# Values projected per pixel row and spread into windows by DRAM transfers, and the norm's square with one PSUM operand, in a fused attention and mixture-of-experts kernel

## The chip, the cores and the metric

The kernel runs on one core of a Trainium2 chip. A core has five engines with a queue each, executed in order: TensorE (PE in the profile; its weight loads are PEld), VectorE (DVE), ScalarE (ACT), GpSimd (POOL) and SyncE (SP), which here only issues transfers (its queue is SPq). Transfers run on 16 DMA engines [...]. The working memory SBUF has 128 partitions; TensorE writes its results to PSUM. The metric is the device time of one execution in microseconds (us). Before the change it is 4484.66 us, the median of three runs (4481.55 to 4487.19). The profiled execution spans 4480.1 us.

## What is computed

The input `x` has the shape (2, 128, 256, 256): two images of 128 channels. A block of attention is added to it, then a block of experts. All is float32. Cut to what matters:

```python
# attention block: windows of 8x8 pixels attend to 12x12 pixels around them, 4 heads of 32
xn  = (x - mean_c(x)) / sqrt(var_c(x) + 1e-6)         # norm over the 128 channels of a pixel
q, k, v = split(W_qkv @ xn)
k, v = unfold_windows(k), unfold_windows(v)           # 12x12 patches with step 8, zeros outside
attn = softmax(q * SCALE @ k.T + rel_pos_emb(q) + FIXED_MASK)
x    = x + W_out @ (attn @ v)
# experts, for each pixel as a token t
t = x.reshape(2, 128, -1).transpose(0, 2, 1)
n = (t - mean(t)) / sqrt(var(t) + 1e-5)
p = softmax(n @ router_w + router_b);  p2, i2 = top_k(p, 2);  p2 = p2 / sum(p2)
out = t + sum_k p2[k] * (n @ expert_w[i2[k]] + expert_b[i2[k]])
```

`FIXED_MASK` removes every second row and every second column offset. So a pixel attends only to pixels of the same parity of row and column: each image falls into four independent planes of half height and half width, and in a plane a window of 4x4 pixels attends to 6x6 pixels. That is why the halo on each side is one pixel of the plane.

## The kernel before

**Tiling.** An image is cut into 32 strips of 8 rows, 64 strips in all. Each strip has four planes (row parity by column parity), 256 planes in all, and the main loop (L779) runs over them. A plane has 4 rows by 128 columns of pixels, 512 tokens, in 32 windows. The window rows of a strip need six plane rows: four of its own and one above and below. Six rows are kept as a ring: `place(i, k)` says in which of six places row `k` of strip `i` lies, and the two rows that two strips share stay where they are. `ln_rows(i)` gives the rows that strip `i` has to bring in anew: rows 2 to 5 inside an image, 1 to 5 in its first strip and 2 to 4 in its last. `runs` groups such rows into stretches of neighbouring places.

**The values.** Two neighbouring windows read 10 columns of the plane (KC): 8 of their own and one of halo on each side. So 16 column groups of 6 x 10 = 60 pixels, in slots of 64, cover the plane, and the halo columns are in two groups each. GpSimd copies the normalized pixels `xn` into this doubled order (`columns`, L331) as `xcol`, with 128 partitions of channels; two groups (half 0 and half 1) stand side by side and fill 128 pixels. TensorE then multiplies each of the eight pairs of groups by `wv` (`values`, L369), four pairs into one PSUM tile, and ScalarE copies the tile into `vv` (L376): pixels on the partitions, channels along the row, as the attention (L496) needs them. Per plane that is eight matmuls of 128x128 by 128x128 and two ScalarE copies. A float32 matmul shows as two records in the trace, so four matmuls are the "x8" in a row of the timeline.

**The keys** are not doubled before the projection: `pk` is projected once per pixel (L396), and ScalarE doubles the halo columns while it copies out of PSUM into `kcol` (L407, L414), which lasts from strip to strip in the ring.

**The order.** The loop is a software pipeline whose order is written out by hand: under `tc.manual_schedule` each engine executes its instructions in the order in which the Python code emits them. Several planes are in work at once. For iteration `n`: scores of plane `n` (L448, L465; exp at L473), the projection of plane `n + 1` (the generator `ahead` = `project`: first value group, `pu`, `pk`, `pq`), the last four expert products of one pixel-row pair (`ex.product`, L686), the attention of plane `n` (L486, L496; division by the sums at L506 to L516), the norm statistics of two later pixel-row pairs (`norms`, L554 to L572), the second value group, three expert products, the output projection `po` (L524, added to `xt` at L529), the fourth product. VectorE's order around the change: the expert multiplies `xe` (L677), `ex.end` (L692), the attention's `sT`, `rc`, `rT`, `o` (L506 to L516), the transposed statistics `plg` (L563), `rstd` (L228 to L235), the gates of the router (`route`, L587 to L619) up to `gT` (L625), then `uT` (L386) and `au` (L354).

**The norm.** `rstd` takes mean and mean square of the pixels from the PSUM tile `plg`, as views `mean` and `sq`. L228 copies the mean to the SBUF tile `r`, L229 squares it, L230 subtracts from `sq`, L231 clamps and adds epsilon (`epsc` lies in SBUF), ScalarE does Ln and Exp (L232, L233), L234 and L235 make a Newton step.

**GpSimd** does, per plane: a marker `last` (L681) that makes it wait for VectorE's sixth expert multiply, expert multiply 5 (L677), the normalization of one pixel-row pair (`ln1`, L272), every fourth plane the copy of a shared row (`halo`, L246), expert multiply 7 (L677), and `columns` of a plane two ahead (L331).

**SyncE** issues all transfers of the loop in order: eight broadcasts of gates per plane (`gb`, L661), one each of `sb` and `rb` (L666, L637), one load of `x` (L115), one store (L722) and two small writes of the gates to DRAM (`gd`, L633), from which `gb`, `sb` and `rb` are read back. The expression `nc.scalar` or `dve` in `fetch` names the engine whose little write into the tile marks when the transfer may start. PSUM has three rotating tiles of one bank for everything that `mm_tile` asks for.

Of the kernel before, what the change touches and what calls it, by code (L numbers as in the profile page):

```python
# [11 lines left out]
F32 = mybir.dt.float32  # L12
AF = mybir.ActivationFunctionType
ALU = mybir.AluOpType
# [3 lines left out]
P = 128  # L18
# [25 lines left out]
KR, KC = 6, 10  # L44
NK = KR * KC
SLOT = 64
# [5 lines left out]
def kernel(  # L52
# [39 lines left out]
    def mm_tile(name):  # L92
        return ps_mm.tile([P, 512], F32, tag="mm", name=name)

    def ctile(shape, name):
        return const.tile(shape, F32, tag=name, name=name)
# [98 lines left out]
    nc.tensor.matmul(pr[:, :P], lhsT=wall[:, 0, :], rhs=relbd, start=True, stop=True)  # L195
    nc.vector.tensor_copy(wrel, pr[:, :P])

    xn, xcol, kcol = [], [], []
    for i in range(2):
        xn.append(ctile([P, 2, 2, KR, PC + 2], f"xn{i}"))  # L200
        nc.gpsimd.memset(xn[i][:, :, :, :, 0 : PC + 2 : PC + 1], 0.0)
    for i in range(4):
        xcol.append(ctile([P, HP, 2, SLOT], f"xcol{i}"))
        kcol.append(ctile([P, NP, SLOT], f"kcol{i}"))
        nc.gpsimd.memset(xcol[i][:, :, :, NK:], 0.0)
        nc.gpsimd.memset(kcol[i][:, :, NK:], 0.0)
        nc.gpsimd.memset(kcol[i][:, 0, 0:NK:KC], 0.0)
        nc.gpsimd.memset(kcol[i][:, NP - 1, KC - 1 : NK : KC], 0.0)
# [9 lines left out]
    def rstd(p4, k0, k1, name):  # L218

        u, r = (
            small.tile([P, 2, NT], F32, tag=v, name=f"{v}_{name}")[:, k0:k1] for v in ("u", "r")
        )
        mean, sq = (
            p4[:, :, E + 2 * k0 + j : E + 2 * k1 : 2].rearrange("p t k -> p k t") for j in range(2)
        )
        nc.vector.tensor_copy(r, mean)  # L228
        nc.vector.tensor_tensor(u, r, r, ALU.mult)  # L229
        nc.vector.scalar_tensor_tensor(u, u, -1.0, sq, ALU.mult, ALU.add)  # L230
        nc.vector.scalar_tensor_tensor(u, u, 0.0, epsc[:, k0:k1], ALU.max, ALU.add)  # L231
        nc.scalar.activation(r, u, AF.Ln, scale=4.0)  # L232
        nc.scalar.activation(r, r, AF.Exp, scale=-0.5)  # L233
        nc.vector.scalar_tensor_tensor(u, u, -4.0, r, ALU.mult, ALU.mult)  # L234
        nc.vector.tensor_tensor(u, u, r, ALU.mult)  # L235
        return r, u

    def ln_rows(i):

        s = strips[i][1]  # L240
        return range(1 if s == 0 else 2, KR - 1 if s == NS - 1 else KR)
# [9 lines left out]
    def place(i, k):  # L251

        return (PR * strips[i][1] + k) % KR

    def runs(i, rows):

        out = []
        for k in rows:
            if out and place(i, k) == out[-1][1] + out[-1][2]:
                out[-1][2] += 1  # L260
            else:
                out.append([k, place(i, k), 1])
        return out
# [59 lines left out]
            ln1(i, k, pb, nc.vector)  # L323
        yield

    def columns(n):

        i, pl = divmod(n, 4)
        for k, at, m in runs(i, ln_rows(i)):
            for half in range(2):  # L330
                nc.gpsimd.tensor_copy(  # L331
                    xcol[pl][:, :, half, at * KC : (at + m) * KC].rearrange(
                        "p t (r c) -> p t r c", c=KC
                    ),
                    windows(xn[i % 2][:, pl // 2, pl % 2, k : k + m], half * HP, HP),
                )
        for k, s in ((0, 0), (KR - 1, NS - 1)):
            if strips[i][1] == s:
                c0 = place(i, k) * KC
                nc.gpsimd.memset(xcol[pl][:, :, :, c0 : c0 + KC], 0.0)  # L340
                nc.gpsimd.memset(kcol[pl][:, :, c0 : c0 + KC], 0.0)

    def shift(uT, n, state):

# [12 lines left out]
    def project(n, state):  # L357
# [1 line left out]
        i, pl = divmod(n, 4)  # L359
        xp = xn[i % 2][:, pl // 2, pl % 2]  # L360
        inner = xp[:, 1 : 1 + PR, 1 : PC + 1]
        xl, kk = xcol[pl], kcol[pl]

        vv = work.tile([P, HP, P], F32, tag="vv", name=f"vv{n}")

        def values(t0):
            pv = mm_tile(f"pvv{n}_{t0}")
            for t in range(4):
                nc.tensor.matmul(  # L369
                    pv[:, t * P : (t + 1) * P],  # L370
                    lhsT=xl[:, t0 + t].rearrange("p a k -> p (a k)"),
                    rhs=wv,
                    start=True,
                    stop=True,
                )
            nc.scalar.copy(vv[:, t0 : t0 + 4, :].rearrange("p t c -> p (t c)"), pv)  # L376

        values(0)
        yield

        pu = mm_tile(f"pu{n}")
        nc.tensor.matmul(pu, lhsT=wrel, rhs=inner, start=True, stop=True)  # L384
# [37 lines left out]
        )  # L422
        yield

        values(4)
        state.update(qs=qs, kk=kk, vv=vv)
        yield

    def windows(rows, n0, count):

        first = rows[:, :, 8 * n0 : 8 * n0 + KC].unsqueeze(1)
        dims = [list(d) for d in first.ap]
        dims[1] = [8, count]
        return bass.AP(first.tensor, first.offset, dims)
# [310 lines left out]
            next(part)  # L745
    if len(strips) > 1:
        halo(1)
    columns(0)
    states = {0: {}}
    for _ in project(0, states[0]):  # L750
        pass
    states[0]["shift"]()
    if n_planes > 1:
        columns(1)

# [20 lines left out]
    with tc.manual_schedule(engines={ET.PE, ET.DVE, ET.Activation, ET.Pool, ET.SP}):  # L778
        for n in range(n_planes + 7):  # L779
# [32 lines left out]
            next(ahead, None)  # L812
            if n + 1 < n_planes:
                states[n + 1]["shift"]()
            next(ahead, None)
            next(ahead, None)
            for e in (4, 6, 7, 5):
# [26 lines left out]
            new.fetch(3, dve)  # L844
            while to_store:
                store(*to_store.pop())
            next(ahead, None)
            ex.product(0)
            made = next(norm, None)
# [8 lines left out]
                halo(i + 2)  # L858
            nxt.times(7, pool)
            if n + 2 < n_planes:  # L860
                columns(n + 2)
            next(outp, None)
            ex.product(3)
            next(outp, None)
# [61 lines left out]
```

The softmax here doesn't subtract the row's maximum and nothing guards it: scores larger than these inputs give would overflow.

## Time and profile before

| what | value |
|---|---|
| time, median of 3 | 4484.66 us |
| VectorE square L229, planes 0 to 259 | 0.16 to 1.30 us, median 0.83, sum 233.0 |
| L228, the copy before it | 0.17 us, sum 44.0 |
| value matmuls L369, 4096 records | 594.3 us busy, 288 ns each |
| ScalarE copy L376, 512 | 299.8 us, 586 ns each |
| GpSimd copy L331, 672 | 237.6 us, 391 ns each |
| GpSimd expert multiply L677, 512 | 650.8 us, 1272 ns each |
| `gb` transfers L661, 2048 of 256 KB | issue 0.32 us, landing after 4.0 |
| `rb` transfers L637, 249 of 256 KB | issue 0.33 us, landing after 3.3 |
| `gd` writes L633, 516 of 16 KB | issue 0.59 us, landing after 3.0 |
| stores L722, 256 of 256 KB | issue 0.43 us, landing after 4.2 |
| DMA packets, main queue | 517,568, 58.3% of the time of 16 engines |

The page gives for each engine the time in which an instruction was running. A busy TensorE is not one at its peak, since matmuls overlap; the time that a group of them holds the engine is read from the start of the first to the start of what follows. The timeline has columns start, duration, engine, line, operation, output and inputs, shapes, and how many instructions were merged; idle time before the instruction and what ended it stand in brackets. A duration includes a wait that arises inside the engine once the instruction has been issued. A wait for a semaphore shows as idle time before it.

### The profile page before, as it was taken

What the parts mean: (1) busy time and instruction counts of PE and PEld (TensorE: products, weight loads), DVE (VectorE), ACT (ScalarE), POOL (GpSimd) and SP (SyncE); (2) the same over time, 40 slices, a digit from 0 to 9 for tenths busy, and PEclk for the clock granted to TensorE, in tenths of its full rate; (3) what the DMA queues carried; (4) which work ended last, traced back from release to release, by engine and by line L of the source; (5) the groups of instructions that cost most, each with busy time, mean ns of one, the idle gap of its engine ahead of it and who ended that gap; (6) DMA issues with size and microseconds to landing.
All of it is one profiled execution on the core that took longest, in us unless ns stands there. A gap on an engine that the chain in (4) does not pass through costs nothing. (4 is left out here: it accounts for less than half of the span.)

```text
span 4480.1 us, 224632 instructions
## 1 busy us (share of the span) xinstructions
PE 4422.6 (99%) x96321; PEld 2683.3 (60%) x96321; DVE 3996.2 (89%) x11850; ACT 1467.7 (33%) x4022; POOL 1317.7 (29%) x1815
## 2 busy tenths in 40 slices
PE   7999999999999999999999999999999999999997
PEld 5666666666666666666666666666666666666653
DVE  5899999999899999998989999999999999989887
ACT  3333333333333333333333333333333333333321
POOL 1232323232323233232323232323232323232321
PEclk9999999999999999999999999999999999999999
DMA  2565666566656666666666566666665666566655
GB/s 83 174 191 185 192 185 192 186 191 185 193 184 192 185 191 187 189 188 188 189 187 189 187 190 185 193 183 193 184 193 185 192 185 192 186 191 186 190 164 186
DMA packets 519284, 828.12 MB, mean 185 GB/s; under 512 B 124186, under 2 KB 125850, under 8 KB 518298
## 3 DMA queue, kind: packets, MB, share of 16 engines
q1 hardware_dynamic: 517568, 813.46, 58.3%
q8 instruction: 769, 12.60, 1.1%
q14 instruction: 217, 1.78, 0.2%
q10 hardware_dynamic: 730, 0.29, 0.0%
HBM read 737.95 MB, written 75.56 MB: 182 GB/s over the span
## 5 line engine op out<-in xcount | busy, mean ns | idle before, releaser
L686 PE MATMUL acc<-xe,ew 128*128 128x512 f32 x4096 | 1889.0, 594 | 19.6 <-DVE gb L660 18.8
L686 PEld LDWEIGHTS acc<-xe,ew 128*128 128x128 f32 x4096 | 758.8, 190 | 885.7 <-issue 861.8
L677 DVE TENSOR_TENSOR xe<-xs,gb 128x512 f32<-128x512 f32 x1536 | 950.9, 687 | 10.2 <-PE acc L686 0.7
L681 POOL COPY last<-xe 128x1 f32<-128x1 f32 x256 | 47.9, 187 | 3060.8 <-DVE gb L660 3054.6
L376 ACT COPY vv<-pvv 128x512 f32<-128x512 f32 x512 | 299.8, 586 | 1395.7 <-PE pvv L369 1379.6
L677 POOL TENSOR_TENSOR xe<-xs,gb 128x512 f32<-128x512 f32 x512 | 650.8, 1272 | 5.9 <-PE att L496 2.5
L369 PE MATMUL pvv<-wt,xcol 128*128 128x128 f32 x4096 | 594.3, 288 | 2.5 <-POOL xcol L331 1.5
L369 PEld LDWEIGHTS pvv<-wt,xcol 128*128 128x128 f32 x4096 | 496.4, 191 | 64.8 <-issue 51.8
L272 POOL TENSOR_TENSOR xn<-xt,rb 128x512 f32<-128x512 f32 x249 | 375.0, 1506 | 66.5 <-DMA rb<-gd 55.9
L465 PE MATMUL att<-qs,kcol 32*64 32x32 f32 x32768 | 392.4, 226 | 0.8 <-issue 0.7
L465 PEld LDWEIGHTS att<-qs,kcol 32*64 32x64 f32 x32768 | 391.0, 130 | 1.0 <-issue 1.0
L496 PEld LDWEIGHTS att<-pT,vv 64*32 64x32 f32 x32768 | 348.0, 105 | 39.4 <-issue 2.5
L496 PE MATMUL att<-pT,vv 64*32 64x32 f32 x32768 | 343.2, 200 | 2.3 <-issue 2.3
L473 ACT ACTIVATE pT<-att 128x1024 f32<-128x1024 f32 x256 | 261.9, 1023 | 243.1 <-PE att L465 239.7
L548 ACT ACTIVATE sq<-xt 128x512 f32<-128x512 f32 x505 | 292.7, 631 | 0.0
L354 DVE STREAM_TRANSPOSE au<-auT 128x512 f32<-128x512 f32 x256 | 269.2, 1052 | 9.0
L524 PE MATMUL po<-o,wt 128*128 128x512 f32 x512 | 262.0, 593 | 6.1 <-DVE o L516 3.2
L384 PE MATMUL pu<-xn,wrel 128*128 128x512 f32 x512 | 262.5, 594 | 0.0
L407 ACT COPY kcol<-pk 128x560 f32<-128x560 f32 (+2 forms) x344 | 174.1, 506 | 268.2 <-PE pk L396 265.3
L418 PE MATMUL pq<-xn,wt 128*128 128x512 f32 x512 | 262.0, 593 | 0.0
L396 PE MATMUL pk<-xn,wt 128*128 128x512 f32 (+2 forms) x528 | 261.0, 578 | 0.0
L386 DVE STREAM_TRANSPOSE uT<-pu 128x512 f32<-128x512 f32 x256 | 182.8, 714 | 78.0 <-PE pu L384 77.0
(2697 smaller groups left out, 5243.8 us busy)
## 6 DMA issues: line engine op xcount, KB each, us to landing
gb<-gd SPq DMA_DIRECT2D x2048, 256.0 KB, 4.0
xt<-in_x_dram SPq DMA_DIRECT2D x256, 256.0 KB, 4.9
sb<-gd SPq DMA_DIRECT2D x256, 256.0 KB, 3.5
out_dram<-xt SPq DMA_DIRECT2D x256, 256.0 KB, 4.2
rb<-gd SPq DMA_DIRECT2D x249, 256.0 KB, 3.3
gd<-gT SPq DMA_DIRECT2D x516, 16.0 KB, 3.0
ew<-in_L_ffn_expert_w_dram SPq DMA_DIRECT2D x1, 512.0 KB, 5.0
eb<-in_L_ffn_expert_b_dram SPq DMA_DIRECT2D x1, 512.0 KB, 5.7
```

What stands on the lines that cost most here:

```text
L272: eng.tensor_tensor(xn[i % 2][:, :, :, k, 1 : PC + 1], ln1_src(i, k).rearrange("p (y j x) -> p y x j", y=2, x=2), rb.rearrange("p (y j x) ...
L354: nc.vector.transpose(au.rearrange("p m a s -> p a s m"), auT[n % 2])
L369: nc.tensor.matmul(pv[:, t * P : (t + 1) * P], lhsT=xl[:, t0 + t].rearrange("p a k -> p (a k)"), rhs=wv, start=True, stop=True,)
L376: nc.scalar.copy(vv[:, t0 : t0 + 4, :].rearrange("p t c -> p (t c)"), pv)
L384: nc.tensor.matmul(pu, lhsT=wrel, rhs=inner, start=True, stop=True)
L418: nc.tensor.matmul(pq, lhsT=wq, rhs=inner, start=True, stop=True)
L465: nc.tensor.matmul(sc[rows, h, 32 * t : 32 * t + 32], lhsT=kk[hp, half * HP + t, :], rhs=qs[hp, m0 : m0 + 2].rearrange("p m a s -> p (m a ...
L496: nc.tensor.matmul(av[hp, half, 32 * t : 32 * t + 32], lhsT=vv[rows, t, hp], rhs=pT[rows, h, 32 * t : 32 * t + 32], start=True, stop=True,)
L524: nc.tensor.matmul(po, lhsT=wo, rhs=state["o"].rearrange("p f z -> p (f z)"), start=True, stop=True)
L548: nc.scalar.activation(sq, src, AF.Square)
L677: eng.tensor_tensor(self.xe[e], self.xs, self.gb.pop(e), ALU.mult)
L686: nc.tensor.matmul(self.acc, lhsT=ew[:, e, :], rhs=self.xe.pop(e), start=(e == 0), stop=not self.xe)
```

## The change

There are two edits.

**Values once per pixel.** `columns`, `xcol` and the second value group go. `value_rows` projects every new plane row once: one matmul per row, with the 128 pixels of the row as stationary operand, so that the pixels come out on the partitions. ScalarE copies the tile to SBUF (`vr`). `send_values` writes it to a DRAM buffer `vrows` (one per plane, six rows in the ring, 130 columns of which the outer two stay zero, 128 channels), and `take_values` reads it back as overlapping windows: for each new row and half one transfer of 10 partitions (columns) by 8 windows by 128 channels, 40 KB in pieces of 512 B, into `vwin`, which stays from strip to strip as `kcol` does. `borders` does what was left of `columns`: zeros for rows outside the image. The purpose is to project no halo pixel twice, and to let the transfers do the doubling that GpSimd did.

**The square.** L229 multiplies the copy `r` by the PSUM view `mean` instead of by itself. The value is the same; one operand is read from PSUM.

```diff
+    zero = ctile([P, 2, P], "zero")
...
     for i in range(4):
-        xcol.append(ctile([P, HP, 2, SLOT], f"xcol{i}"))
+        vwin.append(ctile([P, HP, P], f"vwin{i}"))
         kcol.append(ctile([P, NP, SLOT], f"kcol{i}"))
+        vrows.append(dram.tile([KR, PC + 2, P], F32, tag=f"vrows{i}", name=f"vrows{i}", bufs=1))
+        nc.gpsimd.memset(vwin[i], 0.0)
+        nc.sync.dma_start(vrows[i][:, 0 : PC + 2 : PC + 1, :], zero[0:KR])
...
-        nc.vector.tensor_tensor(u, r, r, ALU.mult)
+        nc.vector.tensor_tensor(u, r, mean, ALU.mult)
...
-    def columns(n):
...
+    def value_rows(n):
+        i, pl = divmod(n, 4)
+        xp = xn[i % 2][:, pl // 2, pl % 2]
+        rows, sent = list(ln_rows(i)), []
+        for part in (rows[-4:], rows[:-4]):
+            if not part:
+                continue
+            pv = mm_tile(f"pv{n}_{part[0]}")
+            m = len(part)
+            for j, k in enumerate(part):
+                nc.tensor.matmul(pv[:, j * P : (j + 1) * P], lhsT=xp[:, k, 1 : PC + 1], rhs=wv,
+                                 start=True, stop=True)
+            vr = work.tile([P, 4, P], F32, tag="vr", name=f"vr{n}_{part[0]}")
+            nc.scalar.copy(vr[:, 0:m].rearrange("p r c -> p (r c)"), pv[:, : m * P])
+            sent.append((part, vr))
+        return sent
+    def send_values(n, sent):
+        i, pl = divmod(n, 4)
+        for part, vr in sent:
+            for k, at, m in runs(i, part):
+                nc.sync.dma_start(vrows[pl][at : at + m, 1 : PC + 1, :].rearrange("r c d -> c r d"),
+                                  vr[:, k - part[0] : k - part[0] + m])
+    def take_values(n):
+        i, pl = divmod(n, 4)
+        s = strips[i][1]
+        for k in range(0 if s == 0 else 2, KR):
+            at = place(i, k)
+            for half in range(2):
+                p0 = half * SLOT + at * KC
+                src = vrows[pl][at, half * HP * 8 : half * HP * 8 + KC, :].unsqueeze(1)
+                dims = [list(d) for d in src.ap]
+                dims[1] = [8 * P, HP]
+                nc.sync.dma_start(vwin[pl][p0 : p0 + KC], bass.AP(src.tensor, src.offset, dims))
...
-        values(0)
-        yield
...
+        state["sent"] = value_rows(n)
+        yield
...
-        values(4)
-        state.update(qs=qs, kk=kk, vv=vv)
+        state.update(qs=qs, kk=kk, vv=vwin[pl])
         yield
...
                 states[n + 1]["shift"]()
+                send_values(n + 1, states[n + 1]["sent"])
...
             while to_store:
                 store(*to_store.pop())
+            if n + 1 < n_planes:
+                take_values(n + 1)
             next(ahead, None)
             ex.product(0)
...
             if n + 2 < n_planes:
-                columns(n + 2)
+                borders(n + 2)
```

So the sends of plane `n + 1` stand in SyncE's queue behind `spread` (`gd` and `rb`) and ahead of `sb`, and its takes behind the store and ahead of the fetches of `gb` 4 and 6.

## The prediction

> **What bounds the kernel now.** I read the busy line first, then one window over the steady stretch, then the waits, then the timeline of single planes. The busy line and the window (columns: length, then busy time of PE, PEld, DVE, ACT, POOL, then clock, DMA share, GB/s):
>
> ```profile
> PE 4422.6 (99%) x96321; PEld 2683.3 (60%) x96321; DVE 3996.2 (89%) x11850; ACT 1467.7 (33%) x4022; POOL 1317.7 (29%) x1815
> ...
> 180.00:4300.00 4120.00, 4119.93 (x90232) 2502.24 (x90231) 3731.25 (x11041) 1371.11 (x3758) 1240.61 (x1670) 1.00 0.61 188
> ```
>
> TensorE has no hole at all, at full clock. VectorE is busy 91% of the stretch (3731/4120), but is it free for the other 9%? The waits answer (engine, line, releaser: us in total, times, longest):
>
> ```profile
> DVE uT L386 <- PE pu L384: 77.0, 186, 7.9
> ...
> DVE sT L506 <- PE att L496: 10.6, 10, 2.6
> ...
> DVE xt L529 <- PE po L524: 3.5, 11, 0.6
> ```
>
> One plane takes 17.17 us: the exps of planes 16 and 240 start at 286.98 and 4133.22, and 3846.24/224 = 17.17. Between them VectorE waited for TensorE 49 us (45.6 for uT, 2.0 for po, 1.4 for the attention), or 0.22 us per plane. Its other idle time is the 0.52 us in each plane for the Ln and Exp of the norm (116 us in all) and the steps from one instruction to the next. So TensorE sets the pace and VectorE follows 0.22 us behind: **two engines bound this kernel**.
>
> One ordinary plane shows what the change touches:
>
> ```profile
> 1017.62 1.16 PE L369 MATMUL pvv<-wt,xcol 128*128 128x128 f32 x8
> 1018.62 2.74 PE L686 MATMUL acc<-xe,ew 128*128 128x512 f32 x6
> 1019.32 1.26 POOL L677 TENSOR_TENSOR xe<-xs,gb 128x512 f32<-128x512 f32 x1
> 1019.57 0.17 DVE L228 COPY r__58_19002<-plg 128x8 f32<-128x8 f32 x1
> 1019.77 0.83 DVE L229 TENSOR_TENSOR u__58_19001<-r__58_19002 128x8 f32<-128x8 f32 x1
> 1020.64 0.16 DVE L230 SCALAR_TENSOR_TENSOR u__58_19001<-u__58_19001,plg 128x8 f32<-128x8 f32 x1
> 1020.84 0.17 DVE L231 SCALAR_TENSOR_TENSOR u__58_19001<-u__58_19001,epsc 128x8 f32<-128x8 f32 x1
> 1024.95 1.16 PE L369 MATMUL pvv<-wt,xcol 128*128 128x128 f32 x8
> 1025.94 1.02 PE L384 MATMUL pu<-xn,wrel 128*128 128x512 f32 x2
> ```
>
> Each value group (four matmuls, eight records) holds TensorE for 1.00 us, start to start of what follows; the median over 244 planes is 0.99 for either group. The square of the mean, eight numbers per partition, takes 0.83 us where its neighbours take 0.16. It ends at 1020.60, and GpSimd's multiply ends at 1020.58. Over planes 6 to 255, 234 of these 250 squares began under that multiply and ended 0.02 us after it. They wait for GpSimd.
>
> [...] L230 has the same shape with one input in PSUM, 0.16 us. [...] here L230 (PSUM) takes 0.16 and L235 (SBUF only) 0.17 us, so I charge nothing.
>
> But L231 (u with epsc) has two SBUF inputs as well. In a plane where the multiply began just after the square:
>
> ```profile
> 1998.21 0.35 DVE L229 TENSOR_TENSOR u__115_37452<-r__115_37453 128x8 f32<-128x8 f32 x1
> 1998.50 1.27 POOL L677 TENSOR_TENSOR xe<-xs,gb 128x512 f32<-128x512 f32 x1
> 1998.60 0.16 DVE L230 SCALAR_TENSOR_TENSOR u__115_37452<-u__115_37452,plg 128x8 f32<-128x8 f32 x1
> 1998.79 1.00 DVE L231 SCALAR_TENSOR_TENSOR u__115_37452<-u__115_37452,epsc 128x8 f32<-128x8 f32 x1
> ```
>
> L231 waits to 1999.79, GpSimd ends at 1999.77. **The wait moves two instructions on.**
>
> **The change part by part.**
>
> TensorE: an inner strip has four rows per plane to project instead of eight window groups, so four of eight value matmuls go: −0.99 us of a gapless engine per plane (the first strip of an image has five rows, the last three). The remaining group stands where the first one stood. New TensorE time: 17.17 − 0.99 = 16.18.
>
> VectorE: without its wait, the square in the plane shown ends at 1019.94, L230 at 1020.14, and L231 begins at 1020.17 and is held to 1020.60. It ended at 1021.01 before, so 0.41 is won of the 0.66 that the square had waited. I worked this through for 244 planes from their own starts and multiply ends: mean 0.435 us, which includes the few squares with nothing to wait for. The 0.22 us of waits for TensorE also go, since TensorE gets up to 0.99 us ahead. New VectorE time: 17.17 − 0.435 − 0.22 = 16.51. That is above 16.18, so VectorE sets the pace.
>
> GpSimd loses the window copies at L331 (237.6 us, 672 copies). They came after its last multiply and nobody waited for them: 0. ScalarE loses one 0.59 us copy per plane and is 33% busy: 0. PSUM: one tile fewer in the rotation of three. The tile for pu now takes over from plg, whose last reader (L595) ended at 1024.01 while pu began at 1025.94; even 1 us earlier it doesn't wait: 0.
>
> SyncE's queue: per plane one or two sends and eight takes (four rows by two halves; twelve in an image's first strip). The issue of one is not in the trace; bounds are 0.32 us (gb) and 0.59 (gd, the most folded pattern). I take 0.4: 3.2 us for the takes, range 2.6 to 4.7. They stand between the output store and gb4, gb6, gb5, gb7, then gd. From the end of the store's issue to the end of route (gT) SyncE has 6.35 us in the median plane, 5.9 after the VectorE saving, and must issue 8 takes and 4 gb: 3.2 + 1.3 = 4.5 (up to 6.0). It fits, mostly into time SyncE spends waiting for markers. The takes wait for the sends[...]; the sends go out right after rb, some 6.5 us before, and a store of 256 KB lands in 4.2. Behind the takes are the gb fetches, needed half a plane later or more, and the next gd. The values land about 4 us after the last take, near 1044.5 for a plane whose attention begins near 1049: hidden.
>
> DMA engines: the steady share 0.61 is 10.5 us per engine and plane. Sends add 512 pieces of 512 B, 32 per engine. Takes add 8 × 80 pieces[...]. The price of a 512 B piece I take from the load of ew at the start (1024 such pieces, then eb in 4 KB pieces):
>
> ```profile
> 11.50:12.50 1.00, 1.00 (x27) 0.93 (x20) 0.00 (x0) 0.00 (x0) 0.00 (x0) 1.00 1.01 274
> 12.50:13.50 1.00, 1.00 (x28) 0.92 (x24) 0.00 (x0) 0.00 (x0) 0.00 (x0) 1.00 1.13 402
> ```
>
> From 11.0 to 14.5 both loads move 1.05 MB. eb alone, at 402 GB/s, needs 1.3 us; that leaves 2.2 us for 64 pieces per engine, 34 ns each (an estimate). [...] The upper bound is the mean packet of the page, 0.583 × 16 × 4480/517,568 = 81 ns.
>
> Start and end: the first planes take 12 us, with room for the takes; I count no gain before plane 7. **Sum:** 0.655 us × 248 planes = 162; 4485 − 162 = **4322**.
>
> **Rivals.**
> 1. TensorE stays the bound: the wait doesn't reappear at L231, for instance because GpSimd's multiply comes earlier. Then VectorE falls to 17.17 − 0.76 − 0.22 = 16.19, level with 16.18, and 0.98 × 248 = 243 gives 4242. Against it: the plane at 1998, and GpSimd starts from a VectorE result, 3.16 us ahead of L228 in the median plane.
> 2. SyncE or the DMA queue delays gd and rb. rb is issued 4.71 us before GpSimd's row multiply begins and lands in 3.3, so 1.4 us are free. Past that, GpSimd's last multiply moves back and L231 with it; 0.44 more and the saving at the norm is gone. What is left is 0.22 × 248 = 55: 4430. For it: takes at 0.59 us leave SyncE no slack.
> 3. [...] Against it: the 34 ns above.
>
> **How the numbers follow.** Forecast 0.60, rival 1 0.14, rival 2 0.14, rival 3 0.12. The range begins at TensorE's bound (4238) and ends at 4400: it takes in two thirds of the way to rival 2, for planes that lose only part. Left out are rival 3 and the worse half of rival 2. Faster: the first two and nearly all of rival 2, 0.86; within 0.2% 0.03; slower 0.11.
>
> **What would show it.** In the changed kernel: planes of 16.5 us; square 0.16 us in every plane; L231 (or its counterpart) at about 0.4 us in most, more where a shared row was copied,, ending with GpSimd's multiply; uT no longer waiting for pu; TensorE with some 0.3 us of idle time per plane, before po or the first expert product; one value group; takes of 0.3 to 0.6 us and a DMA share near 0.75. It is wrong if GpSimd waits for rb in most planes, if TensorE waits for vwin, or if gb lands far later than its 4.0 us.

## The result and the profile after

| | before | after |
|---|---|---|
| time, median | 4484.98 us | 5232.2 us (5151.62 to 5334.05) |
| ratio, 95% interval | | 1.1564 [1.1484, 1.1643] |
| TensorE busy | 4422.6 us, 99% | 4573.2 us, 86% |
| TensorE instructions | 96,321 | 94,273 |
| packets of the main DMA queue | 517,568, 58.3% | 843,720, 61.8% |

The change made the kernel slower by 16 to 17%, where 4322 us was forecast. The four runs after it scatter by some 3.5%. Where runs scatter this much (here, in e4 and in e6), the ratio is that of the fastest ones alone, here 5151.62 and 5221.9, and not that of the medians. The profiled execution is the longest of the four, 5332.2 us in the trace.

The busy line of the page after, two of its groups (line, engine, operation, count, busy time and mean in ns, then the idle time before and what ended it), and the second group as it was before the change (L272):

```profile
PE 4573.2 (86%) x94273; PEld 2630.6 (49%) x94273; DVE 4000.9 (75%) x11850; ACT 1305.3 (24%) x3774; POOL 1088.4 (20%) x1128
...
L525 PE MATMUL att<-pT,vwin 64*32 64x32 f32 x32768 | 379.8, 204 | 624.8 <-issue 624.2
...
L276 POOL TENSOR_TENSOR xn<-xt,rb 128x512 f32<-128x512 f32 x249 | 372.8, 1497 | 504.5 <-DMA rb<-gd 458.1
...
L272 POOL TENSOR_TENSOR xn<-xt,rb 128x512 f32<-128x512 f32 x249 | 375.0, 1506 | 66.5 <-DMA rb<-gd 55.9
```

TensorE has fewer instructions and more busy time: its granted clock was lower, 0.917 in the mean of this execution. And 624 us of holes stand ahead of matmuls of the attention, L525. "issue" means that no semaphore that the profile shows ended them. GpSimd waits for rb in 174 planes, 458.1 us in all; before the change it was 55.9 us, in 4 planes. The stretch that showed TensorE gapless before, and three short ones:

```profile
180.00:4300.00 4120.00, 3581.52 (x74343) 2059.00 (x74342) 3162.72 (x9294) 1024.10 (x2971) 861.73 (x865) 0.92 0.64 188
4395.00:4396.00 1.00, 1.00 (x4) 0.38 (x2) 1.00 (x3) 0.00 (x0) 0.00 (x0) 1.00 0.00 0
4397.00:4402.00 5.00, 1.01 (x111) 0.90 (x98) 1.44 (x5) 0.00 (x0) 4.04 (x5) 0.90 1.00 237
4401.00:4404.00 3.00, 1.85 (x53) 1.68 (x56) 1.15 (x3) 0.00 (x0) 1.58 (x2) 0.50 0.73 269
```

TensorE falls from 4119.93 to 3581.52 of 4120 us, the mean clock to 0.92; just after a hole it is granted 0.50. One such plane in the timeline:

```profile
4392.91 3.59 PE L715 MATMUL acc<-xe,ew 128*128 128x512 f32 x8
4396.44 0.66 PE L515 MATMUL att<-pT,ones 64*32 64x256 f32 x16
4396.89 1.12 PE L525 MATMUL att<-pT,vwin 64*32 64x32 f32 x103
4402.15 0.44 PE L525 MATMUL att<-pT,vwin 64*32 64x32 f32 x25 [4.14 <-issue]
```

The hole is in the middle of one loop, 103 matmuls done and 25 to go, though the first of them already had all their operands. Why there? Counted from the first score of its plane, the instruction after the hole is number 608 in 166 of 167 planes with such a pause. An alignment of TensorE's instructions, written into the loop (L824) with BLOCK = 256 and FIRST_LIMIT = 95, puts ends of blocks of 256 at 95, at 351 (the first expert product) and at 607. In both traces each of planes 10 to 247 has 768 of TensorE's records, three times 256. The DMA queue named "instruction" holds 769 packets of 16 KB in both kernels, three per plane, and one lands in the pause. By these counts **TensorE stands at a block boundary without its next instructions.**

One packet is then one block, 16 KB for 256 instructions. In the kernel before, its load is hidden: the packet of the block wanted at 607 comes 1.1 us after TensorE crosses 351, and 607 is reached 4.9 us after that crossing. It is so in the 71 planes after the change without a pause (1.6 us). In the 167 others it comes 6.4 us after the crossing: TensorE is at 607 by then, and goes on 1.4 us after the packet's end. Traffic alone didn't hold it off: from 4395 to 4396 in the window above the DMA engines moved nothing.

Planes without a pause take 16.4 us, planes with one 22.4. The kernel without takes (e1 below) has the same TensorE instructions and no pause; its busy time is 4234.5. The difference of the two spans, 5332.2 − 4371.9 = 960 us, is thus, within 3 us, 624 us of pauses and 4573.2 − 4234.5 = 339 us of lower clock. That says where the time of this execution lies, and not yet why.

SyncE's order changed as well. Waits of the kernel after (total, times, longest):

```profile
POOL xn L276 <- DMA rb<-gd: 458.1, 174, 27.8
...
SPq L666 <- DMA gd<-gT: 700.8, 249, 4.6
...
SPq L385 <- DMA gb<-gd: 454.3, 692, 2.5
...
SPq L385 <- DMA xt<-in_x_dram: 92.8, 172, 1.7
SPq L385 <- DMA out_dram<-xt: 68.4, 189, 1.9
```

L385 is a take. It needs neither gates nor x nor the output, yet waits for their transfers. The transfers of SyncE report on eight semaphores, numbers 101 to 108 in the trace, that are used in turn (6028 of its 6031 steps from one transfer to the next). The eight issued ahead of the takes are one send, sb, gb0, gb1, gb2, xt, gb3 and the store, and the waits have this composition: four gb (692) to one xt (172) and one store (189). **Each take waits for the transfer eight places before it.**

### The profile page after: what moved, and what is told of

Read it like the earlier page. It is cut to its first block, busy times and chain, and to the rows that moved or that the text cites. A ratio compares the mean times of both kernels' runs of the same rounds, so it can differ in the third digit from the quotient of the medians.

```text
span 5332.2 us, 226269 instructions
## 1 busy us (share of the span) xinstructions
PE 4573.2 (86%) x94273; PEld 2630.6 (49%) x94273; DVE 4000.9 (75%) x11850; ACT 1305.3 (24%) x3774; POOL 1088.4 (20%) x1128
## 3 DMA queue, kind: packets, MB, share of 16 engines
q1 hardware_dynamic: 843720, 966.94, 61.8%
## 5 line engine op out<-in xcount | busy, mean ns | idle before, releaser
L715 PE MATMUL acc<-xe,ew 128*128 128x512 f32 x4096 | 2132.1, 656 | 67.0 <-issue 44.8
L715 PEld LDWEIGHTS acc<-xe,ew 128*128 128x128 f32 x4096 | 843.0, 212 | 1139.6 <-issue 1087.5
L525 PE MATMUL att<-pT,vwin 64*32 64x32 f32 x32768 | 379.8, 204 | 624.8 <-issue 624.2
L525 PEld LDWEIGHTS att<-pT,vwin 64*32 64x32 f32 x32768 | 361.8, 108 | 682.6 <-issue 643.1
L535 DVE STREAM_TRANSPOSE sT<-att 128x512 f32<-128x512 f32 x256 | 183.4, 716 | 572.0 <-PE att L525 570.6
L276 POOL TENSOR_TENSOR xn<-xt,rb 128x512 f32<-128x512 f32 x249 | 372.8, 1497 | 504.5 <-DMA rb<-gd 458.1
L558 DVE TENSOR_TENSOR xt<-po,xt 128x512 f32<-128x512 f32 x256 | 176.2, 688 | 219.1 <-PE po L553 219.0
L350 PE MATMUL pv<-wt,xn 128*128 128x128 f32 x2048 | 301.1, 290 | 1.4 <-issue 1.4
L583 PE MATMUL plt<-sq,rw 128*32 128x128 f32 x4040 | 271.3, 350 | 4.3 <-issue 4.3
L583 PE MATMUL plt<-xt,rw 128*32 128x128 f32 x4040 | 269.0, 348 | 0.0
L621 ACT ACTIVATE lg<-lg 128x32 f32<-128x32 f32 x256 | 58.7, 229 | 853.8 <-DVE lg L620 853.8
```

Source lines behind the costliest of these rows:

```text
L276: eng.tensor_tensor(xn[i % 2][:, :, :, k, 1 : PC + 1], ln1_src(i, k).rearrange("p (y j x) -> p y x j", y=2, x=2), rb.rearrange("p (y j x) ...
L350: nc.tensor.matmul(pv[:, j * P : (j + 1) * P], lhsT=xp[:, k, 1 : PC + 1], rhs=wv, start=True, stop=True,)
L525: nc.tensor.matmul(av[hp, half, 32 * t : 32 * t + 32], lhsT=vv[rows, t, hp], rhs=pT[rows, h, 32 * t : 32 * t + 32], start=True, stop=True,)
L583: nc.tensor.matmul(plt[32 * t : 32 * t + 32, :P], lhsT=rw[:, j], rhs=src[:, t * P : (t + 1) * P], start=(j == srcs[0][0]), stop=(j == srcs ...
L715: nc.tensor.matmul(self.acc, lhsT=ew[:, e, :], rhs=self.xe.pop(e), start=(e == 0), stop=not self.xe)
```

## The experiments

**e1 to e4: which part.** e1 and e2 leave out takes or sends, e3 is the other half of the change alone, e4 moves the block boundaries by six instructions (three matmuls).

```
e1 (after):   - take_values(n + 1)                     in the loop
e2 (after):   - send_values(n + 1, ...)                in the loop
e3 (before):  - tensor_tensor(u, r, r, ALU.mult)
              + tensor_tensor(u, r, mean, ALU.mult)
e4 (after):   - BLOCK, FIRST_LIMIT = 256, 95
              + BLOCK, FIRST_LIMIT = 256, 101
```

> The changed kernel without the takes in the loop (the attention then reads windows that hold zeros; the sends stay). Theory F, instruction blocks: the takes and the gate fetches that pile up behind them keep the DMA engines busy just when TensorE's next block of 256 instructions has to be loaded; the block comes late and TensorE stands still in the attention at L525. Without takes no plane stalls, all planes take the 16.4 us of the changed kernel's unstalled planes, 4484 - 0.8 x 248 = about 4290 us. Rival W, the sends with their 512-byte pieces into DRAM are what fills the engines: still above 4900. Rival S, SyncE's order (gd and rb late, GpSimd waits for rb) costs the time: also about 4290, since the takes no longer hold the queue.

> The changed kernel without the sends in the loop (the DRAM rows are zeroed once at the start and the takes read zeros). Theory F: the takes alone hold SyncE for 3 to 7 us per plane and push the gate fetches together, so most stalls stay: 4800 to 5250 us. Rival W: the stalls go with the sends, about 4290. Rival S: as theory F, since the takes stay.

> The kernel before with the square's edit alone. By the prediction VectorE gets 0.435 us per plane more slack but TensorE, which is unchanged, sets the pace: within 10 us of 4485, with L231 at 0.4 us or more in most planes. If VectorE's chain had been part of the bound, up to 100 us less.

> The changed kernel with the constant that aligns TensorE's instruction stream set to 101 instead of 95: each boundary between blocks of 256 instructions lies three matmuls later in the plane, the transfers and all work are the same. Theory F: the first block boundary after the scores has 1.3 us more and the next 1.3 us less time to be loaded, so the number of stalled planes (167 of 238) and the time change clearly, by over 150 us in one direction; the better guess is fewer stalls, 4500 to 5000. Rivals W and S: nothing in the transfers or in SyncE's queue differs, so 5230 within 2%.

A pause is counted here where more than 1.2 us pass in the attention from the start of one matmul to that of the next, and the profile names "issue".

| | time, us | ratio to before, 95% | paused planes, of 238 |
|---|---|---|---|
| e1, no takes | 4376.0 | 0.9743 [0.9719, 0.9766] | 0 |
| e2, no sends | 5131.4 | no interval | 142 |
| e3, square only | 4483.1 | 0.9989 [0.9982, 0.9995] | not counted |
| e4, boundary +6 | 5265.6 | 1.1622 [1.153, 1.1714] | 157 |

The takes bring the whole loss: e1 is 856 us below the changed kernel by the medians, and 776 below its fastest run. The sends alone don't, since e1 keeps them and is faster than the kernel before; without them (e2) 142 planes still pause. e1 shows what the rest of the change gives, in the stretch that was gapless before:

```profile
180.00:4300.00 4120.00, 4049.77 (x90621) 2366.52 (x90619) 3687.05 (x11355) 1258.01 (x3604) 1039.63 (x1053) 1.00 0.70 209
```

TensorE is 98% busy at full clock. Its planes take 16.36 us in the median, 16.6 in the mean. e4 is a miss for the theory that only the boundary's place is unlucky: the pause moved with it, to instruction 614. e1 came out 86 us above what was expected of it, and e3 within its range.

**e5 to e8: what about the takes.** Their bytes, TensorE's waits on them, SyncE's order, or the moment?

```
e5 (after):  take into a tile aside that nothing reads; the attention reads vwin
e6 (after):  - vwin[pl][p0 : p0 + KC]    <- 10 pixels x 8 windows
             + vwin[pl][p0 : p0 + 1, 0]  <- one pixel, one window
e7 (after):  - nc.sync.dma_start(vwin ...)
             + nc.scalar.dma_start(vwin ...)
e8 (after):  take_values(n + 1) moved behind new.fetch(4, nc.scalar)
```

> All eight takes per plane are issued as in the changed kernel and move the same pieces, but land in a tile that nothing reads; the attention reads windows of zeros, so the values are left out of the result and TensorE has no semaphore waits on the takes. Theory W (TensorE's four extra wait instructions per plane, for the takes, are what holds back the request for the next 16 KB block of its instructions): as without takes, about 4376 us, under 10 stalled planes of 238. Theory T (the takes' transfers hold it back: their pieces, or SyncE's order around them): as the changed kernel, 5100 to 5300 us, 130 to 180 stalled planes with a pause of some 3.8 us in L525.

> The eight takes keep their place and TensorE waits for each, but each moves one piece of 512 B in place of 80; the rest of the windows stays zero, so most values are left out of the result. Theory W (waits): 5100 to 5300 us, over 130 stalled planes. Theory T in the form that the pieces count: about 4376 us, under 10 stalled planes. Theory S (SyncE's own order and its waits of takes for transfers eight before, whatever they move): 5000 us or more, since eight takes still stand ahead of the gb fetches.

> The takes are issued by ScalarE at the same place of the program, not by SyncE; everything else is as in the changed kernel. Theory S (SyncE's order): near 4376 us plus what ScalarE's eight issues of about 0.3 us cost, below 4450, few stalled planes. Theory T (pieces beside the request for the block): 5000 to 5300 us, over 100 stalled planes.

> The takes are issued by SyncE behind the fetch of gate 4, some 2 to 4 us later than in the changed kernel; the same transfers. Theory T with time (a block is asked for late where pieces run at or before TensorE's second block boundary): the pieces then fall behind that boundary, fewer than 80 stalled planes and below 4800 us. Theory T without time (pieces anywhere in the plane do it): 5100 to 5300 us.

| | time, us | ratio to before, 95% | paused planes |
|---|---|---|---|
| e5, TensorE waits for no take | 5050.7 | 1.1271 [1.1249, 1.1293] | 2 |
| e6, one piece each | 5045.9 | 1.1164 [1.1108, 1.122] | 140 |
| e7, issued by ScalarE | 5097.4 | 1.1369 [1.135, 1.1388] | 0 |
| e8, later | 5030.8 | 1.122 [1.1197, 1.1242] | 146 |

Four times nearly the same time, for three different reasons. e6 settles most of the bytes: with one eightieth of them 140 planes still pause, and the ratio falls only from 1.156 to 1.116. e8 meets neither of its theories: with the takes behind the fetch of gate 4 as many planes pause, so moving them by that much doesn't help, and yet the time is 150 to 200 us lower. e5 fits neither theory as I had put it. The pause all but goes (L525, now L527, waits 6.4 us in all), and the time stays:

```profile
DVE xe L708 <- DMA gb<-gd: 310.9, 272, 5.0
...
POOL xn L278 <- DMA rb<-gd: 793.6, 228, 27.7
...
SPq L668 <- DMA gd<-gT: 743.9, 249, 4.7
SPq L387 <- DMA gb<-gd: 704.4, 966, 2.3
SPq L387 <- DMA xt<-in_x_dram: 121.5, 229, 2.1
SPq L387 <- DMA sb<-gd: 99.4, 184, 1.4
SPq L387 <- DMA out_dram<-xt: 81.0, 214, 1.5
```

With TensorE's waits out of the way, SyncE is nearly filled: the takes (L387) wait 1006 us in these four lines, gates land late, and VectorE and GpSimd wait for gb and rb. (The lines of e5 and e2 stand two further down than in the changed kernel.) There are **two costs in the takes**, and what is left without TensorE's waits on them is still worth 5051 − 4376 = 675 us.

e7 misses in a third way. SyncE idles again, 9.6 us per plane waiting for other engines, but ScalarE's takes stand in its queue ahead of the logarithm of the norms. The timeline of one plane (ACTq is ScalarE's issuing):

```profile
2506.14 0.28 ACTq L385 DMA_DIRECT2D vwin<-vrows  x1
...
2510.56 8.75 ACTq L385 DMA_DIRECT2D vwin<-vrows  x10
2519.35 0.21 ACT L236 ACTIVATE r__127_41488<-u__127_41487 128x8 f32<-128x8 f32 x1 [12.82 <-DMA vwin<-vrows]
```

VectorE waits for that logarithm and its exp: 3.73 us per plane ahead of L238, 0.51 in e1. The surplus is 3.2 × 256 = 820 us, more than e7 loses against e1 (721 us).

**e9 to e11: the number of transfers.** e9 orders the keys of a window column by column, in DRAM, key columns and mask alike. Then the six rows of a half are one transfer, two takes per plane. e10 keeps eight takes but spreads them. e11 has nothing of the change: eight transfers of 512 B each are added to the kernel before.

```
e9 (after):    - vrows [KR, PC + 2, P];  key at*KC + c
               + vrows [PC + 2, KR, P];  key c*KR + at
               + for half in range(2): nc.sync.dma_start(
               +     vwin[pl][half*SLOT : half*SLOT + NK], <60 x 8 x 128 of vrows>)
e10 (after):   a third of the takes each at the old place, behind fetch(4), behind fetch(6)
e11 (before):  + for k in range(8):
               +     nc.sync.dma_start(aside[k : k + 1], spare[k : k + 1])   behind the store
```

> The windows' keys are ordered column by column and no longer row by row (DRAM rows, key columns and the constant mask alike), so that all six rows of a half are one transfer: two takes per plane in place of eight, with half as many bytes again (960 pieces of 512 B in place of 640). The whole result is computed. Theory N (it is the number of SyncE's transfers that costs: each issue, and each wait for the transfer eight before it): SyncE keeps some 7.2 us of issues as without takes, plus 0.7, and few waits; 4376 to 4450 us, below both kernels, under 30 stalled planes. Theory B (bytes or pieces beside other transfers): 5000 us or more, since there are more of them.

> The same eight takes, but in three groups: a third at the old place, a third behind the fetch of gate 4, a third behind that of gate 6. Theory N with waits (most of the loss is SyncE waiting, at a take, for the transfer eight before it, some 2.6 us per plane): these have landed by then or are waited for while SyncE idles anyway; below 4700 us. Theory N with issues and counts alone: 4950 to 5100 us, as before.

> The kernel before with eight transfers of one 512 B piece per plane added at the place of the takes, from a DRAM tensor of zeros to a tile that nothing reads. Theory N: SyncE, with 5.9 us of issues and 2.0 us of waits on transfers per plane before, gets 1.8 us of issues and 3 to 4 us of waits more, in all some 13 of 17.4 us; nothing saturates but gates land later: 4500 to 4750 us, slower than before. If what was harmful is tied to the changed kernel alone (its sends, its DRAM windows, its waits on TensorE): 4480 to 4500 us.

| | time, us | ratio to before, 95% | paused planes |
|---|---|---|---|
| e9, two takes | 4678.3 | 1.0436 [1.042, 1.0451] | 24 |
| e10, spread | 5701.3 | 1.2702 [1.2677, 1.2728] | 227 |
| e11, before + 8 small transfers | 4696.6 | 1.0469 [1.045, 1.0488] | 12 |

e11 isolates the number of transfers: 4 KB per plane, read by nobody, cost 213 us, and the waits are those of the takes.

```profile
SPq L642 <- DMA gd<-gT: 842.6, 249, 4.9
SPq L854 <- DMA gb<-gd: 747.5, 981, 2.6
SPq L854 <- DMA out_dram<-xt: 179.4, 248, 2.1
SPq L854 <- DMA xt<-in_x_dram: 105.0, 246, 1.2
...
POOL xn L277 <- DMA rb<-gd: 499.8, 234, 25.0
```

The last line points to the way from there to the time: rb lands late in 234 planes, and GpSimd's multiplies then run later, where they can hold other instructions of the norm, as the multiply at 1998.50 in the prediction holds L231 for 1.00 us. VectorE is busy for 4237.6 us here and for 3996.2 before, with the same 11,850 instructions; most of the 241 us lie in the norms. That this is the whole of the 213 us is not shown.

e11 came out within the range expected of it. e9, with more bytes and fewer transfers, wins back 554 us of the changed kernel's loss, but stays above the 4450 that I had expected at most. Part of the 554 is the pause, which all but goes as well; against e5, where that is so too, two takes in place of eight win 372 us. e10 is the largest miss, and the most useful: SyncE waits little for transfers here, and idles for VectorE, while TensorE pauses in nearly every plane.

```profile
PE att L529 <- issue: 872.7, 236, 5.6
...
SPq L694 <- DVE plg L596: 1185.5, 244, 8.6
SPq L670 <- DMA gd<-gT: 475.5, 249, 4.3
...
SPq L694 <- DMA gb<-gd: 100.1, 161, 1.8
```

So the pause doesn't come from a filled SyncE. What e10, e6 and e8 have and e5, e9 and e11 lack are separate wait instructions of TensorE just ahead of L525, for the takes: 4 per plane in the changed kernel, e2, e6 and e8, 2 in e10. In e9 two waits go with the matmuls themselves. (e7 has 3 and doesn't pause, but TensorE there takes 2.3 us longer to the boundary at 351 and has the block by then. So the waits alone are not enough.)

**e12 to e14: take TensorE's waits away.** In e12 and e14 ScalarE copies the windows into another tile ahead of the expert products, and TensorE reads that.

```
e12 (e10), e14 (e13):  + nc.scalar.copy(vv, vwin[pl])    the attention reads vv
e13 (e9):              the first take behind fetch(4), the second behind fetch(6)
```

> As e10 (eight takes in three groups), but ScalarE copies the windows into another tile ahead of the attention (some 1.0 us by the exp of the same width), and TensorE reads that tile: it waits for ScalarE and for no take. The whole result is computed. Theory W2 (TensorE's separate waits on the takes bring the pause at the block boundary): the pause goes, SyncE idles as in e10, and the plane falls to 16.5 to 17.5 us: 4350 to 4600 us in place of 5701. Theory T2 (takes that run beside the end of a plane bring the pause, whoever waits): 5500 us or more, over 150 paused planes.

> As e9 (two takes per plane), with the first behind the fetch of gate 4 and the second behind that of gate 6. TensorE waits for both, on its matmuls and not in separate wait instructions. The whole result is computed. Theory N with W2: SyncE waits less for transfers eight before (1.7 us per plane in e9 at the gate fetches), no pause: 4370 to 4500 us. Theory T2: pauses in most planes, 5000 us or more. Neither: as e9, 4680 us.

> As e13, with ScalarE's copy of e12 between takes and attention. Theory N with W2: 4370 to 4500 us as e13, since the copy lies in ScalarE's idle time; if waits on the matmuls themselves bring the pause as well, e13 shows it and this one does not.

| | time, us | ratio to before, 95% | paused planes |
|---|---|---|---|
| e12, e10 with the copy | 4934.3 | 1.1017 [1.0972, 1.1062] | 0 |
| e13, e9 spread | 4697.2 | 1.0466 [1.0448, 1.0483] | 32 |
| e14, e13 with the copy | 4688.3 | 1.0448 [1.0425, 1.0472] | 3 |

e12 against e10 is the cleanest pair: the same transfers, one more instruction on ScalarE, 227 pauses become none, and 767 us go. The copy doesn't only cover the load: the packet of the block comes about 2.5 us after TensorE crosses 351 here and about 6 us after it in e10 (medians), so it starts earlier. But the time stays above the range that I had given. TensorE waits for the copy in 195 planes, ScalarE for the takes, and SyncE is filled as soon as TensorE no longer holds it up:

```profile
PE att L538 <- ACT vv L517: 335.7, 195, 4.3
...
SPq L679 <- DMA gd<-gT: 527.3, 249, 4.1
SPq L703 <- DMA gb<-gd: 491.0, 542, 2.3
SPq L389 <- DMA gb<-gd: 183.9, 480, 2.0
```

e13 and e14 miss as well: spreading two takes, or copying behind them, leaves the time of e9, which was the case "neither" of e13.

The pauses counted so far are those in the attention. The block wanted at 351 comes late too, at the first expert product. These are waits of TensorE in e5, e12 and e14 (in e1 the waits for acc with "issue" are 8.6 us in all):

```profile
PE acc L717 <- issue: 168.1, 184, 2.5
...
PE acc L728 <- issue: 134.8, 137, 2.5
...
PE acc L724 <- issue: 133.8, 190, 2.4
PE att L534 <- ACT vv L513: 120.0, 119, 2.7
```

At exactly that boundary TensorE stands for over 0.5 us in 130 planes of e5, 103 of e12, 153 of e9 and 121 of e14, and in 3 of e1. In none of e5, e12 and e14 does it wait for a take itself, so separate waits are not the only thing that makes a block late. In e11, where nothing of the change is in, 53 planes have such a stop at the boundary at 607, 0.9 us in the median. No run isolates the cause of these shorter stops.

SyncE per plane (sums over the trace divided by 256 planes; the mean plane is that of planes 10 to 247):

| us per plane | issuing | waiting for transfers | together | mean plane |
|---|---|---|---|---|
| before | 5.9 | 2.0 | 7.9 | 17.2 |
| e1, no takes | 7.2 | 2.1 | 9.3 | 16.6 |
| after | 10.5 | 5.5 | 16.1 | 20.6 |
| e5, no TensorE waits | 11.0 | 7.0 | 18.0 | 19.4 |
| e12, spread, no TensorE waits | 11.6 | 6.0 | 17.6 | 19.0 |
| e11, before + 8 | 8.9 | 7.5 | 16.4 | 18.0 |
| e14, two takes, no TensorE waits | 8.5 | 6.4 | 14.9 | 17.8 |
| e10, spread, paused | 10.0 | 2.6 | 12.7 | 22.1 |

Where the long pause is absent and eight transfers were added (e5, e12, e11), SyncE is taken for all but 1.4 to 1.6 us of the plane. In e10 it has 9.4 us to spare.

**e15 and e16: two takes out of SyncE's order.** They are also an attempt at a version below both kernels.

```
e15 (e9):   - nc.sync.dma_start(vwin ...)
            + nc.scalar.dma_start(vwin ...)
e16 (e15):  + the copy of e12
```

> As e9 (two takes per plane, the whole result), but ScalarE issues the two takes at the old place of the program, where it idles some 9 us in e13's trace before the logarithm of the norms. Theory N (SyncE's order): SyncE is as without takes, 4370 to 4450 us, below both kernels. Theory B2 (bytes on the DMA engines, 75%, late loads of TensorE's block): 4600 to 4720 us, as e9 and e13, with some 190 waits of 0.7 us at the first accumulation.

> As e15 with ScalarE's copy of the windows ahead of the attention (TensorE waits for no take). Theory N: 4370 to 4450 us, within 0.5% of e15. Theory B2: 4600 to 4720 us.

4965.7 us (1.1065 [1.1046, 1.1085]) and 4971.1 (1.1085 [1.1068, 1.1101]): both theories miss. The transfers of both queues take their semaphores from one set: at the start of the kernels before and after, the four that ScalarE issues have 103, 105, 107 and 108, and SyncE's first four 101, 102, 104 and 106. A gate fetch of SyncE (L690), eight transfers behind a take that ScalarE issues late, now waits for it in 242 planes, 4.0 us each (e15):

```profile
SPq L690 <- DMA vwin<-vrows: 968.7, 242, 6.7
SPq L666 <- DMA gd<-gT: 520.9, 249, 4.2
```

As in e7, the takes also stand ahead of the logarithm on ScalarE: VectorE waits 567 us in all for it and its exp, 134 in e9, which is 1.7 us per plane more. And TensorE's waits for acc with "issue" come to 284.8 us, 181.5 in e9. How the loss against e9 is shared among the three isn't shown. Another queue is thus no way out while the order of completion is shared. In e14, where neither cost is at its full size, 1.2 us per plane are left above e1. Its trace shows where: TensorE waits 134 us for the block at 351 and 120 us for the copy, together 1.0 us per plane. What makes both late stays open: the bytes (76.5% of the DMA time, 67.8% in e1), or SyncE's 6.4 us of waits. No version of the change that computes the whole result ran below the kernel before; of the change only the square is worth keeping, and its gain, 0.1%, is at the edge of what can be measured.

## Why the prediction was wrong, step by step

- **What bounds the kernel: right.** TensorE and VectorE are close together in e3 and e1. e3 wins on VectorE and gains 0.1%.
- **The square and L231: right.** In e3 the square goes from 0.897 to 0.161 us in the mean of all 260, and L231 from 0.226 to 0.539: 0.42 us won per plane, where 0.435 was worked out. A part of the wait moves on past L231, which the prediction didn't look at: L234 goes from 0.168 to 0.269 us and L235 from 0.167 to 0.185, so that 0.30 is left in e3. After the change the wait stands at L235, as here (the timeline of VectorE after):

```profile
2026.09 0.16 DVE L233 TENSOR_TENSOR u__99_32387<-r__99_32388,plg 128x8 f32<-128x8 f32 x1
2026.28 0.16 DVE L234 SCALAR_TENSOR_TENSOR u__99_32387<-u__99_32387,plg 128x8 f32<-128x8 f32 x1
2026.48 1.23 DVE L235 SCALAR_TENSOR_TENSOR u__99_32387<-u__99_32387,epsc 128x8 f32<-128x8 f32 x1
```

Which of the norm's instructions are held shows in the two traces. Of those with all inputs in SBUF, L229 before the change began 206 times under a TENSOR_TENSOR of GpSimd that had over 0.2 us to go, and L235, L238 and L239 after it 237 times: all but one of these 443 ended 0.02 to 0.03 us after it, and the longest took 1.50 us. L232 to L234, which read PSUM, began under one 258 times after the change and took 0.17 us at most. The cause of the difference isn't shown.

- **The engines' plane of 16.51 us: right.** Planes without a pause take 16.4 after the change; e1 takes 16.36 in the median and 16.6 in the mean, so 4376 and not 4322. Some planes of e1 still wait for pu, 112.7 us in all, which the sum had put at nothing.
- **Copies of GpSimd and ScalarE, PSUM tiles, sends: right** at no cost that shows in e1, which has them all.
- **SyncE's queue: the step that failed first.** "It fits" compared time to issue with time to spare: 4.5 of 5.9 us. The issue was sized well, 2.7 us per plane for the takes against 3.2. What was missing is the wait ahead of each issue. I let takes wait for sends alone; each also waits for the transfer eight places before, at the moment when these are gates on their way for 4 us. Waiting for transfers went from 2.0 to 5.5 us per plane, to 7.0 with TensorE out of the way. The kernel before shows 14 transfers per plane and no such wait among its largest, since eight places back is more than half of them; with 23 it is a third, and the transfer there is still under way. The first sign of being wrong that it gave came true: GpSimd waits for rb in most planes, 174. Rival 2 named this victim, gd and rb, but its cost was cut off at "the saving at the norm is gone": 4430. e11 and e5 show that it doesn't stop there: in e11 VectorE's time grows by 241 us, and in e5 GpSimd waits 793.6 us for rb.
- **Values landing early, so hidden: true of the data, wrong of the cost.** Even after the change no large wait for vwin shows on TensorE (1.1 us in all at L525). What cost is that TensorE has to check: with the wait instructions ahead of L525 the packet of the block comes 5 us late (6.4 us after the crossing of 351 in paused planes, 1.6 in the others), and with the waits moved to ScalarE (e12) it doesn't. No step of the prediction looked at TensorE's instruction stream, although the alignment stands in the loop. In the changed kernel the two costs lie over each other: practically all of the 960 us are in pauses and lost clock, yet without TensorE's waits (e5) only 182 us come back, since SyncE takes over.
- **DMA engines: right to doubt.** A 512 B piece took 27.8 ns in the mean, below the 34 that I estimated and far from 81. The share of 0.64 looks like less than the 0.75 that was forecast, but its plane is longer: 0.64 of 20.6 us is 13.2 us per engine, where 0.75 of 16.5 would be 12.4. Rival 3, DMA engines that are full, ends on the right side, slower, by luck: it can't be the main cause, since most of the loss stays in e6 with a single piece per take. How a take's pieces are spread over the 16 engines was assumed, and no trace shows it.

What is settled: takes cost by their number (e11; e5 against e9), with SyncE's order filled, and by TensorE's separate waits on them, through the long pause (e12 against e10, e5 against e6). That SyncE's order is what turns the number into time is argued from its waits and from rb landing late; no run took these waits away and left the transfers as they were. What stays open is why the packet then starts only when TensorE already stands (1.3 us after it stops, in the median), and why the one at 351 is late without any such wait. The wait instructions themselves pass in 0.05 us each. That fewer of them (e10) pause more often than four has no explanation here either; nor did I try waits without any transfers behind them.

## What to carry to other kernels

Cost an added transfer by its place in the order of completion: look up which transfer stands as many places before it as there are semaphores in turn (eight here), and whether that one has landed by then. Bytes and issue time can both be small and the order full (in e11 4 KB and 3.0 us more per plane, and SyncE taken for 16.4 of 18.0 us). Before a busy engine is made to wait for several transfers of its own, let an idle engine take them and pass on one result: in e12 one copy on ScalarE (an estimate: 1 us, from the 1.02 of the exp of the same width) removed 767 us (with two takes, whose waits go with the matmuls, it removed nothing: e14 against e13). And where "issue" stands behind idle time in the middle of one loop, count instructions to the block boundary before looking for an operand.

## What was not expected of the hardware

- A pause at an instruction block lasted 3.8 us in the median. The block's packet takes 0.95 us; the rest is its start (1.3 us after TensorE stops) and 1.4 us from its end to the next matmul.
- The granted clock fell to 0.50 at such a pause. The trace after the change has 175 stretches at 0.50, 889 us in all, and 173 of them last 3.4 or 6.8 us; the trace before has five, 32 us in all. They come with short pauses too: at 54 of the 64 pauses between 1.0 and 3.0 us ahead of L525 such a stretch began within 5 us of the pause's start. So a pause of 3.8 us cost about 6 us of plane (22.4 against 16.4). The group L715 shows it over the whole run: a matmul takes 656 ns in the mean after the change, 600 without takes (e1).
- The issue of a take took 0.29 us in the median. In the same kernel a gate fetch, with an unchanged pattern, rose from 0.32 to 0.41 in the mean, and to 0.46 in e11, which adds eight small transfers and nothing else. So an added transfer cost more than its own issue; why isn't shown.
